# Group norm and attention on one core: the first normalising in two steps, copies of att in older bursts, and a product with v between two score tiles

## The chip, the core and the metric

The kernel runs on one core of one Trainium2 chip, in one launch. The metric is the device time of one execution in microseconds (us); lower is better. "Before" and "after" are compared by the medians of several executions.

## What is computed

```python
b, c, hh, ww = x.shape                  # 4, 512, 48, 48
t = hh * ww                             # 2304
d = c // num_heads                      # 64, with 8 heads
hn = _group_norm(x, gn_scale, gn_bias)  # 32 groups of 16 channels
qkv = jnp.einsum('oc,bchw->bohw', qkv_w, hn) + qkv_b[None, :, None, None]
qkv = qkv.reshape(b, 3, num_heads, d, t).astype(jnp.float16)
q, k, v = (qkv[:, 0], qkv[:, 1], qkv[:, 2])
scale = jnp.asarray(1.0 / math.sqrt(math.sqrt(d)), dtype=jnp.float16)
w = jnp.einsum('bhct,bhcs->bhts', q * scale, k * scale)
w = jax.nn.softmax(w, axis=-1)
a = jnp.einsum('bhts,bhcs->bhct', w, v).astype(jnp.float32)
a = a.reshape(b, c, hh, ww)
out = jnp.einsum('oc,bchw->bohw', proj_w, a) + proj_b[None, :, None, None]
return x + out
```

## The kernel before, in words

**Tiles.** The 512 channels are four chunks of 128 partitions (c = 0 to 3, `NC`). The 2304 positions are five query blocks (j = 0 to 4, `NQ`): four of 512 columns and a last one of 256. Two heads make a pair; there are four pairs to a batch and 16 pairs g in all. `hn[b, c, j]` holds x, and is normalised in place. All of the work is written out by hand in `fast_path`; each engine runs its instructions in the order in which they are issued there. (`general_path` is a fallback that doesn't run with these inputs.)

**The main loop.** `stream` lists 432 bursts (g, j, k). A burst is three score tiles `ps` of 128 x 1024: TensorE multiplies q and k of both heads (`scores`, L998), ScalarE takes the exponential of each tile into `p` (L1005). There are three `ps` buffers, so a score tile of one burst waits for the exponential of the tile with the same number in the burst before. Two bursts later (`BEHIND`) TensorE multiplies p with v (`values`, L1023) into the one PSUM bank `av`. VectorE adds the p of a block up (`add`, L1054; `join`, L1059). When a block (six bursts, or three for the short one) has ended, `avx` is copied out of the bank (L1032), the sums over keys are made in the same bank (`add_up`, L1082), copied out (`rows`, L1098), inverted and spread by DMA (L1101 to L1139), and GpSimd multiplies to give `att`, 16 bit (`divide`, L1147). For the last blocks of the whole kernel the division is done in place (`divide_here`, L1108 and L1109).

**Work beside the loop.** `beside` is a list of pieces in a planned order: projections to q and k (`qk_steps`, L748, evacuated by VectorE at L758), to v (`v_chain`, L799, L807), and the output projection of the batch before (`proj_run`, L887, with weights as a high and a low part, evacuated with bias and residual at L914, or at L910 where only the last pair's part is added, and stored at L919). They share one PSUM bank. `fill(n)` issues pieces as credit allows, each with an earliest burst (`after`); pieces of up to 0.1 us need no credit. It first runs `do_tasks`: small tasks of a loaded batch, with an allowance of 0 to 2.4 us to a burst: statistics (L621), `aggregate` (L625), `group_scale` (L635 to L647, and the power on GpSimd, L644), `coefficients` (L654 to L666) and `normalize` (L699).

**Copies of att.** The output projection needs `att` as 32 bit: `att32` makes four copies a block (one a pair), ScalarE the first two (L881) and GpSimd the last two (L879); where a `divide` was issued in the same burst, ScalarE makes three. They are issued at a block's `begin` piece. For blocks 2, 3 and 4 of the last batch (`in_two`) three pairs are projected early (`FIRST`: six matmuls a chain) and the last pair later (`LAST`). In the kernel before, `put_run(att32, b, j, FIRST, after=there)` copies all three pairs of such a block just ahead of its chains.

**Start.** While x is loaded, L1317 keeps TensorE busy with matmuls on ones. `all_stats(0)` takes the statistics of chunk 0; `first_group` (L678 to L691) averages them over the groups with two small matmuls on TensorE, raises to the power -1/2 on GpSimd (L686), and makes scale `ga` and bias `gb`. `norm_chunk` (L706) then normalises the five blocks of a chunk on ScalarE, block 0 first. Eight chains (k of five blocks, q of three) go through the chunks together, each in its own bank; the statistics of the next chunk stand among the coefficients of this one on VectorE.

**The last blocks.** `soon` holds the ends of blocks 2 and 3 of the last pair. After the loop come the last block's sums and the remaining chains of the output projection ("ahead", "rest", "held", "last_av").

Of the kernel before, what the change touches and what calls it, by code (L numbers as in the profile page):

```python
# [467 lines left out]
def fast_path(  # L468
# [201 lines left out]
    def first_group():  # L670

        mean, var = moments[:, 1, 0:1], moments[:, 2, 0:1]
        by = share.rearrange("p g j -> p (g j)")
        pm = small_bank("first_group")
        dev, var2, mg, veps, rstd = (
            small_tile(1, f"first_{n}") for n in ("dev", "var2", "mg", "veps", "rstd")
        )
        nc.tensor.matmul(pm[:, 0:1], by, mean, start=True, stop=True)  # L678
        nc.vector.tensor_tensor(dev, mean, pm[:, 0:1], ALU.subtract)
        nc.vector.tensor_scalar(var2, dev, dev, var, ALU.mult, ALU.add)  # L680
        nc.tensor.matmul(pm[:, 1:2], by, var2, start=True, stop=True)
        nc.vector.scalar_tensor_tensor(
            mg, pm[:, 0:1], -1.0, gsc[:, 0:1], ALU.mult, ALU.mult
        )
        nc.vector.tensor_scalar(veps, pm[:, 1:2], EPS, None, ALU.add)
        nc.gpsimd.tensor_tensor(rstd, veps, mhalf[:, 0:1], ALU.pow)  # L686

        def finish():
            ga, gb = small_tile(1, "first_ga"), small_tile(1, "first_gb")
            nc.vector.tensor_tensor(ga, rstd, gsc[:, 0:1], ALU.mult)  # L690
            nc.vector.tensor_scalar(gb, rstd, mg, gbi[:, 0:1], ALU.mult, ALU.add)  # L691
            ab[0, 0] = ga, gb

        return finish
# [5 lines left out]

    def norm_chunk(b, c):

        ga, gb = ab[b, c]
        for j in range(NQ):
            t = hn[b, c, j]
            nc.scalar.activation(t, t, AF.Identity, bias=gb, scale=ga)  # L706

# [156 lines left out]
    def att32(b, j, pairs=range(NC)):  # L867
        o, n = QBLOCKS[j]
        for c in pairs:
            if left_over(b, j):  # L870
                t = xpool.tile([P, n], F32R, tag=f"x{c}_{j}", name=f"a32_{b}_{j}_{c}")
            else:
                t = work.tile(
                    [P, QB], F32R, tag=f"a32_{c}", bufs=1, name=f"a32_{b}_{j}_{c}"
                )
            at32[b, j, c] = t[:, :n]
            source = atts[b * NPAIR + c][:, o : o + n]
            if c in beside_exps() and not (pairs == LAST and left_over(b, j)):
                nc.gpsimd.tensor_copy(at32[b, j, c], source)  # L879
            else:  # L880
                nc.scalar.copy(at32[b, j, c], source)  # L881
# [55 lines left out]
    def proj_pieces(b, j):  # L937
# [7 lines left out]
        def begin():  # L945
            att32(b, j, LAST if in_two(b, j) else range(NC))
            if j == 0:
                ahead(0)
                ahead(1)
# [36 lines left out]
    def scores(u):  # L986
# [5 lines left out]
        for r in range(BURST):  # L992
            ps = ps_s.tile([P, 2, QB], F32, tag="ps", name=f"ps_{g}_{j}_{k}_{r}")
# [172 lines left out]
    def reload(b, j):  # L1166


        def run():
# [4 lines left out]
            if j == NQ - 1:  # L1174

                tasks.append((n, 0.65, lambda: aggregate(b)))
                tasks.append((n, 1.2, lambda: group_scale(b)))
# [12 lines left out]
    def do_tasks(room):  # L1190
        while tasks and tasks[0][0] <= now[0] and room > 0:
            _, us, run = tasks.popleft()
            run()
            room -= us

# [35 lines left out]
    def put_first(b, j):  # L1231

        for jj, chunks in proj_list:
            if jj == j:
                put([proj_piece(b, j, chunks, FIRST)])

    for b in range(B):
# [20 lines left out]
        if b == B - 1:  # L1258
# [4 lines left out]

            ahead = [
# [4 lines left out]
            ]  # L1269
            for j in range(NQ):  # L1270
                put_proj(old, j, ahead)
                if j + 1 < NQ:
                    put_convert(old, j + 1)

            for j in (NQ - 2, NQ - 3, NQ - 1):
                there = ends[(NG - 2) * NQ + j] + BEHIND + 6
                put_run(att32, b, j, FIRST, after=there)
                put_first(b, j)
# [34 lines left out]
    idle = ps_av.tile([P, QB], F32, tag="av", name="idle")  # L1313

    def keep_busy(count):
        for _ in range(count):
            nc.tensor.matmul(  # L1317
                idle, busy[:, 0, :P], busy[:, 0, :], start=True, stop=True
            )

    def all_stats(c):
        for j in range(NQ):
            stats(0, j, c)
        aggregate(0, (c,))

    keep_busy(16)
    all_stats(0)
    first_coefficients = first_group()
    keep_busy(4)

    eight = [(1, j) for j in range(NQ)] + [(0, j) for j in range(8 - NQ)]
# [10 lines left out]
    for c in range(NC):  # L1342

        for j in range(NQ):
            if j == (1 if c < 2 else 2):
                if c == 0:
                    first_coefficients()
                else:
                    coefficients(0, (c,))
                norm_chunk(0, c)  # L1350
            if c + 1 < NC:
                stats(0, j, c + 1)
        if c + 1 < NC:
            aggregate(0, (c + 1,))
            group_scale(0, (c + 1,))
# [75 lines left out]
    for n in range(end):  # L1431
# [5 lines left out]
        scores(stream[n])  # L1437
# [6 lines left out]
        if summed:  # L1444

            fill(n)
        if n >= BEHIND:
# [9 lines left out]
        if not summed:  # L1457
# [158 lines left out]
```

## Time and profile before

| what | value |
|---|---|
| median of three runs | 1601.38 us (1600.72, 1601.38, 1603.44) |
| the profiled execution's own time | 1602.89 us |
| its span | 1601.2 us |
| TensorE: matmul busy | 1583.9 us (99%), 11524 instructions |
| ScalarE busy | 1268.1 us (79%) |
| VectorE busy | 1137.0 us (71%) |
| GpSimd busy | 327.9 us (20%) |
| granted TensorE clock, mean | 0.998 |

Times in the profile count from the start of the span. PE is TensorE (PEld its weight loads), ACT ScalarE, DVE VectorE, POOL GpSimd, SP SyncE, which issues DMAs. A row of the timeline gives start, time, engine, line, operation, output<-inputs, shapes and count; in brackets stands how long the engine had been idle, and what released it. Rows are merged where instructions of one kind follow each other. The end of a matmul is modelled, so the distance from one start to the next is the better measure for PE.

### The profile page before, as it was taken

The numbers are of one execution on the slowest core, as the hardware profiler recorded it, in microseconds if no ns is written. First come the engines' busy times: TensorE is split into PE (matmuls) and PEld (weight loads), VectorE is DVE, ScalarE is ACT, GpSimd is POOL, SyncE is SP. The second block draws the span as 40 slices with busy tenths as digits, with TensorE's granted clock in tenths as the row PEclk, the third lists the DMA queues.
The fourth block names the chain that finished last, engine by engine and source line by source line (L and its number), as shares of the span: only waits on it lengthen the run. The fifth ranks groups of instructions, "written<-read, shape, count | busy, mean of one in ns | idle before, by whom it ended". The sixth has DMA issues, their size and how long they took to land.

```text
span 1601.2 us, 28364 instructions
## 1 busy us (share of the span) xinstructions
PE 1583.9 (99%) x11524; PEld 695.0 (43%) x11524; DVE 1137.0 (71%) x1298; ACT 1268.1 (79%) x1362; POOL 327.9 (20%) x460
## 2 busy tenths in 40 slices
PE   9999999999999999999999999999999999999997
PEld 3533434443333534555333354445533334435554
DVE  6177668876666678887666666888767776766775
ACT  3177777888888888888888888877878888888895
POOL 1011212222121222222112111222212121111322
PEclk9999999999999999999999999999999999999999
DMA  7002020000000024521000001353101000015424
GB/s 217 8 14 67 11 71 17 18 15 12 14 18 15 9 70 119 145 64 28 11 15 18 14 12 41 111 154 90 25 15 18 15 15 11 15 31 163 151 67 128
DMA packets 94896, 82.10 MB, mean 51 GB/s; under 512 B 50852, under 2 KB 60964, under 8 KB 94756
## 3 DMA queue, kind: packets, MB, share of 16 engines
q1 hardware_dynamic: 92724, 78.35, 18.1%
q8 instruction: 92, 1.51, 0.4%
q10 hardware_dynamic: 1904, 1.84, 0.4%
q14 instruction: 48, 0.39, 0.1%
q0 software_dynamic: 128, 0.01, 0.0%
HBM read 60.70 MB, written 19.17 MB: 50 GB/s over the span
## 4 chain that ended last, share of the span: by engine, by line
PE 96%; DVE 1%; ACT 1%; DMA 1%; POOL 0%; issue 0%; SPq 0%; DVEq 0%
PE pqk L748 29%; PE ps L998 20%; PE av L1023 20%; PE pv L799 15%; PE pr L887 8%; PE sl L1082 2%; PE ps L748 1%; ACT p L1005 1%; DMA x<-x_dram 0%; DMA r<-x_dram 0%; DVE acc L1054 0%; PE first_av L748 0%; PE first_w L748 0%; DVE st L621 0%; POOL a L879 0%
## 5 line engine op out<-in xcount | busy, mean ns | idle before, releaser
L1005 ACT ACTIVATE p<-ps 128x1024 f16<-128x1024 f32 x1296 | 1233.3, 1025 | 302.5 <-PE ps L998 299.5
L1054 DVE TENSOR_TENSOR acc<-acc,p 128x3072 f16<-128x3072 f16 x270 | 487.2, 1805 | 54.0 <-ACT p L1005 51.6
L748 PE MATMUL pqk<-x,wqkv 128*64 128x512 f32 (+1 forms) x2432 | 510.2, 549 | 0.1
L1023 PE MATMUL av<-p,v 128*64 128x512 f16 (+1 forms) x2880 | 360.8, 364 | 0.4 <-DVE slx L1098 0.3
L998 PE MATMUL ps<-q,k 64*128 64x512 f16 (+1 forms) x2880 | 356.2, 358 | 1.5 <-ACT p L1005 1.1
L799 PE MATMUL pv<-wqkv,x 128*64 128x256 f32 x2304 | 267.5, 379 | 0.0
L748 PEld LDWEIGHTS pqk<-x,wqkv 128*64 128x64 f32 x2432 | 168.0, 137 | 205.9 <-issue 156.2
L1120 POOL TENSOR_SCALAR in<-sums 128x8 f32<-128x8 f32 (+1 forms) x158 | 101.3, 641 | 723.8 <-DMA sums<-slx 717.2
L998 PEld LDWEIGHTS <-k 64*128 64x128 f16 x2880 | 106.0, 94 | 288.5 <-issue 239.6
L1023 PEld LDWEIGHTS <-v 128*64 128x64 f16 x2880 | 131.3, 109 | 213.3 <-issue 168.6
L1147 POOL TENSOR_TENSOR att<-avx,ib 128x512 f16<-128x512 f32 (+1 forms) x78 | 126.5, 1622 | 434.2 <-DMA ib<-row 372.4
L799 PEld LDWEIGHTS pv<-wqkv,x 128*64 128x64 f32 x2304 | 161.7, 137 | 85.4
L1054 DVE TENSOR_TENSOR acc<-p,p 128x3072 f16<-128x3072 f16 x79 | 138.1, 1748 | 0.0
L887 PE MATMUL pr<-a,whi 128*128 128x512 f32 (+1 forms) x311 | 121.9, 399 | 2.6 <-DVE r L914 2.2
L1059 DVE TENSOR_TENSOR acc<-acc 128x1024 f16<-128x1024 f16 x156 | 112.5, 721 | 3.3
L887 PE MATMUL pr<-a,wlo 128*128 128x512 f32 (+1 forms) x311 | 113.6, 373 | 0.0
L758 DVE TENSOR_SCALAR k<-pqk,bqkv 128x512 f16<-128x512 f32 (+1 forms) x75 | 52.1, 695 | 77.4 <-PE pqk L748 77.2
L807 DVE TENSOR_TENSOR v<-pv,bv 128x512 f16<-128x512 f32 x72 | 49.6, 689 | 80.9 <-PE pv L799 80.8
L758 DVE TENSOR_SCALAR q<-pqk,bqkv 128x512 f16<-128x512 f32 (+1 forms) x77 | 53.4, 694 | 74.6 <-PE pqk L748 74.4
L1098 DVE COPY slx<-sl 128x512 f32<-128x512 f32 (+1 forms) x79 | 50.6, 640 | 66.0 <-PE sl L1082 66.0
L914 DVE SCALAR_TENSOR_TENSOR r<-pr,bproj,r 128x512 f32<-128x512 f32 (+1 forms) x80 | 54.9, 694 | 45.3 <-PE pr L887 40.2
L1032 DVE COPY avx<-av 128x512 f32<-128x512 f32 (+1 forms) x79 | 50.6, 640 | 38.5 <-PE av L1023 38.1
(102 smaller groups left out, 498.6 us busy)
## 6 DMA issues: line engine op xcount, KB each, us to landing
r<-x_dram SPq DMA_DIRECT2D x72, 256.0 KB, 3.6
out_dram<-r SPq DMA_DIRECT2D x69, 256.0 KB, 2.7
ib<-row SPq DMA_DIRECT2D x126, 128.0 KB, 3.1
x<-x_dram SPq DMA_DIRECT2D x62, 256.0 KB, 4.1
x<-x_dram SPq DMA_DIRECT2D x16, 128.0 KB, 5.0
sums<-slx SPq DMA_DIRECT2D x128, 2.0 KB, 2.1
ib<-row SPq DMA_DIRECT2D x30, 64.0 KB, 2.9
wqkv<-qkv_wT_dram SPq DMA_DIRECT2D x2, 768.0 KB, 6.9
```

What stands on the lines that cost most here:

```text
L748: nc.tensor.matmul(pw[0][lo : lo + D, :n], wqkv[:, c, w0 + lo : w0 + lo + D], hn[b, c, j], start=(c == 0), stop=(c == NC - 1),)
L758: nc.vector.tensor_scalar(qk[g][part][:, o : o + n], pw[0][:, :n], bqkv[:, col : col + 1], SCALE, ALU.add, ALU.mult,)
L799: nc.tensor.matmul(pw[0][lo : lo + D, a, :], hn[b, c, i * P // QB][:, at + lo : at + lo + D], wqkv[:, c, 2 * C + half * C // 2 :][:, : C / ...
L887: nc.tensor.matmul(ps[:, :n], w[:, c, bass.ts(m, P)], at32[b, j, c], start=(i == 0), stop=(i == len(steps) - 1),)
L914: nc.vector.scalar_tensor_tensor(xt[:, i], places[i], bias, xt[:, i], ALU.add, ALU.add)
L998: nc.tensor.matmul(ps[:, h, a * n : (a + 1) * n], kt[rows, bass.ts(i, P)], qt[rows, o : o + n], start=True, stop=True,)
L1005: nc.scalar.activation(pt[:, r], ps, AF.Exp)
L1023: nc.tensor.matmul(av[0][lo : lo + D, :n], vv[b, pr // 2][:, i, pr % 2 * P + lo : pr % 2 * P + lo + D], pt[:, r, h, a * n : (a + 1) * n], ...
L1054: nc.vector.tensor_tensor(t, before, pt, ALU.add)
L1059: nc.vector.tensor_tensor(t[:, 0], t[:, 0], t[:, r], ALU.add)
L1120: nc.gpsimd.tensor_scalar(t, sm, limit, None, op)
L1147: nc.gpsimd.tensor_tensor(atts[g][:, o : o + n], avx.pop((g, j))[:, :n], ibs.pop((g, j))[:, :n], ALU.mult,)
```

## The change

Five parts. In the start, `first_group` takes the mean of the variances by a matmul of its own, ahead of the deviations, and normalises in two steps: block 4 (256 columns) and block 0 of chunk 0 are multiplied by the channel's scale with the mean taken off while the power is still being computed, and by the power after it, block 4 on VectorE, block 0 on ScalarE; blocks 1 to 3 are done in one step as before. `next_group` does so with block 4 of the other chunks, on ScalarE. Chains and blocks start with block 4. The statistics of the next chunk come after all of this chunk's coefficients.

In the last batch, the copies of pairs 0 and 1 of blocks 3, 2 and 4, and of pair 2 of block 3, become pieces between the chains of the batch before; pair 2 of blocks 2 and 4 and pairs 0 and 1 of block 0 follow among the `FIRST` chains, those of block 0 on GpSimd. Pairs 0 and 1 of block 2 get tiles of their own.

`do_tasks` stops ahead of `group_scale` if a copy is due among the next two pieces.

In the loop, the product with v of the burst that ends block 3 of the last pair is issued between the second and the third score tile of a burst; and in the bursts that follow the two ends in `soon`, `fill` comes ahead of `values`.

```diff
-    def first_group():
+    def scale_bias(c, tag, col, mg):
+        ga, gb = (small_tile(1, f"{n}_{tag}") for n in ("ga", "gb"))
+        nc.vector.tensor_tensor(ga, col, gsc[:, c : c + 1], ALU.mult)
+        nc.vector.tensor_scalar(gb, col, mg, gbi[:, c : c + 1], ALU.mult, ALU.add)
+        ab[0, c] = ga, gb
+
+    def shifted(c, tag, mean):
+        mg = small_tile(1, f"mg_{tag}")
+        nc.vector.scalar_tensor_tensor(
+            mg, mean, -1.0, gsc[:, c : c + 1], ALU.mult, ALU.mult
+        )
+        return mg
+
+    def by_scalar(t, scale, bias):
+        nc.scalar.activation(t, t, AF.Identity, bias=bias, scale=scale)
+
+    def by_vector(t, scale, bias):
+        nc.vector.tensor_scalar(t, t, scale, bias, ALU.mult, ALU.add)
+
+    def first_group(meanwhile):
...
+        nc.tensor.matmul(pm, by, mean, start=True, stop=True)
+        nc.tensor.matmul(pv, by, var, start=True, stop=False)
+        nc.vector.tensor_tensor(dev, mean, pm, ALU.subtract)
+        nc.vector.tensor_tensor(dev2, dev, dev, ALU.mult)
+        nc.tensor.matmul(pv, by, dev2, start=False, stop=True)
+        mg = shifted(c, "a", pm)
+        small_first, then = hn[0, c, NQ - 1], hn[0, c, 0]
+        by_scalar(small_first, gsc[:, c : c + 1], mg)
+        by_scalar(then, gsc[:, c : c + 1], mg)
+        nc.vector.tensor_scalar(veps, pv, EPS, None, ALU.add)
         nc.gpsimd.tensor_tensor(rstd, veps, mhalf[:, 0:1], ALU.pow)
...
+        meanwhile()
+        by_vector(small_first, rstd, gbi[:, c : c + 1])
+        by_scalar(then, rstd, gbi[:, c : c + 1])
+        scale_bias(c, "a", rstd, mg)
+        for j in range(1, NQ - 1):
+            by_scalar(hn[0, c, j], *ab[0, c])
+
+    def next_group(c):
...
+        aggregate(0, (c,))
...
+        nc.gpsimd.tensor_tensor(rstd, veps, mhalf, ALU.pow)
+        means, mean_cols = small_tile(SQ, "means"), small_tile(SQ, "mean_cols")
+        nc.vector.tensor_copy(by_group(means), to_channels(grouped[:, :, 0]))
+        nc.vector.transpose(mean_cols, means)
+        mg = shifted(c, tag, mean_cols[:, c : c + 1])
+        first = hn[0, c, NQ - 1]
+        by_scalar(first, gsc[:, c : c + 1], mg)
+        scales, cols = small_tile(SQ, "scales"), small_tile(SQ, "cols")
+        nc.vector.tensor_copy(by_group(scales), to_channels(rstd))
+        nc.vector.transpose(cols, scales)
+        by_scalar(first, cols[:, c : c + 1], gbi[:, c : c + 1])
+        scale_bias(c, tag, cols[:, c : c + 1], mg)
+        for j in range(NQ - 1):
+            by_scalar(hn[0, c, j], *ab[0, c])
...
-    def att32(b, j, pairs=range(NC)):
+    EARLY = range(2)
+
+    def att32(b, j, pairs=range(NC), beside=None):
...
+            elif in_two(b, j) and c in EARLY:
+                t = xpool.tile(
+                    [P, n], F32R, tag=f"x{2 * c + 1}_1", name=f"a32_{b}_{j}_{c}"
+                )
...
-            if c in beside_exps() and not (pairs == LAST and left_over(b, j)):
+            if beside or c in beside_exps() and not (pairs == LAST and left_over(b, j)):
...
-            att32(b, j, LAST if in_two(b, j) else range(NC))
+            if in_two(b, j):
+                att32(b, j, LAST)
+            elif (b, j) == (B - 1, 0):
+                att32(b, j, range(len(EARLY), NC))
+            else:
+                att32(b, j)
...
-    def scores(u):
+    def scores(u, ahead_of_last=None):
...
         for r in range(BURST):
+            if r == BURST - 1 and ahead_of_last:
+                ahead_of_last()
...
-                tasks.append((n, 1.2, lambda: group_scale(b)))
+                power = lambda: group_scale(b)
+                powers.add(power)
+                tasks.append((n, 1.2, power))
...
     def do_tasks(room):
         while tasks and tasks[0][0] <= now[0] and room > 0:
+            if tasks[0][2] in powers and copies_next():
+                break
...
+    def copies_next():
+
+        return any(p[0] == 0.0 and p[5] <= now[0] for p in beside[:2])
...
-    def put_first(b, j):
+    def put_first(b, j, ahead):
 
         for jj, chunks in proj_list:
             if jj == j:
+                if ahead:
+                    put_run(*ahead.pop(0))
                 put([proj_piece(b, j, chunks, FIRST)])
...
+            THIRD = range(len(EARLY), NC - 1)
...
+            ahead += [
+                (att32, b, j, (c,)) for j in (NQ - 2, NQ - 3, NQ - 1) for c in EARLY
+            ]
+            ahead.append((att32, b, NQ - 2, THIRD))
             for j in range(NQ):
                 put_proj(old, j, ahead)
...
+            ahead = [
+                (att32, b, NQ - 3, THIRD),
+                (att32, b, NQ - 1, THIRD),
+                *((att32, b, 0, (c,), True) for c in EARLY),
+            ]
             for j in (NQ - 2, NQ - 3, NQ - 1):
-                there = ends[(NG - 2) * NQ + j] + BEHIND + 6
-                put_run(att32, b, j, FIRST, after=there)
-                put_first(b, j)
+                put_first(b, j, ahead if j != NQ - 2 else [])
...
-    eight = [(1, j) for j in range(NQ)] + [(0, j) for j in range(8 - NQ)]
+    first_group(meanwhile)
+
+    eight = [(1, j) for j in (NQ - 1, *range(NQ - 1))] + [(0, j) for j in range(8 - NQ)]
...
     for c in range(NC):
-
-        for j in range(NQ):
-            if j == (1 if c < 2 else 2):
-                if c == 0:
-                    first_coefficients()
-                else:
-                    coefficients(0, (c,))
-                norm_chunk(0, c)
-            if c + 1 < NC:
-                stats(0, j, c + 1)
         if c + 1 < NC:
-            aggregate(0, (c + 1,))
-            group_scale(0, (c + 1,))
+            for j in range(NQ):
+                if (j, c) != (0, 0):
+                    stats(0, j, c + 1)
+            next_group(c + 1)
...
-        scores(stream[n])
+        inside = n - BEHIND == soon[1]
+        scores(stream[n], (lambda: values(stream[n - BEHIND])) if inside else None)
...
-        if summed:
+        filled = summed or n - BEHIND - 1 in soon
+        if filled:
 
             fill(n)
-        if n >= BEHIND:
+        if n >= BEHIND and not inside:
             values(stream[n - BEHIND])
...
-        if not summed:
+        if not filled:
             fill(n)
```

## The prediction

> **What bounds the kernel.** I read the page first, then the waits of PE, then the starts in PE's timeline.
>
> ```profile
> span 1601.2 us, 28364 instructions
> ...
> PE 1583.9 (99%) x11524; PEld 695.0 (43%) x11524; DVE 1137.0 (71%) x1298; ACT 1268.1 (79%) x1362; POOL 327.9 (20%) x460
> ...
> PE 96%; DVE 1%; ACT 1%; DMA 1%; POOL 0%; issue 0%; SPq 0%; DVEq 0%
> ```
>
> PE is both the busy engine and the chain. The change removes no useful matmul, so it can gain only where PE stands still. The waits of PE name the places:
>
> ```profile
> PE pr L887 <- DVE r L914: 2.2, 1, 2.2
> ...
> PE ps L748 <- ACT x L706: 1.3, 1, 1.3
> PE ps L998 <- ACT p L1005: 1.1, 3, 0.5
> ...
> PE pr L887 <- POOL a L879: 0.4, 1, 0.4
> PE av L1023 <- DVE slx L1098: 0.3, 1, 0.3
> ...
> PE sl L1082 <- DVE avx L1032: 0.2, 1, 0.2
> ```
>
> The first row (at 1047 us) is a residual's DMA that lands late, behind loads of x. SP's queue holds the same instructions in the same order in both kernels, so I leave these 2.2 us. The others are what the change aims at. The timelines show them; first the start, with what leads to the first chain:
>
> ```profile
> 9.80 0.58 POOL L686 TENSOR_TENSOR first_rstd<-first_veps,mhalf 128x1 f32<-128x1 f32 x1 [4.69 <-DVE first_veps L685]
> ...
> 10.80 3.42 ACT L706 ACTIVATE x<-x,first_gb,first_ga 128x512 f32<-128x512 f32 x5 [4.60 <-DVE first_gb L691]
> ...
> 11.67 4.94 PE L748 MATMUL ps<-x,wqkv 128*64 128x512 f32 x24 [1.34 <-ACT x L706]
> ```
>
> then the power that stands ahead of a copy on POOL,
>
> ```profile
> 1067.35 0.71 POOL L644 TENSOR_TENSOR rstd<-veps,mhalf 128x2 f32<-128x2 f32 x1 [0.30 <-DVE both L647]
> 1068.02 2.12 POOL L879 CAST a<-att 128x512 fp32r<-128x512 f16 x1
> ```
>
> and three ACT copies in one gap with the score tile that waits for them, the product that waits for `slx`, and the third score tile among short bursts:
>
> ```profile
> 1512.73 1.67 ACT L881 CAST a<-att 128x512 fp32r<-128x512 f16 x3
> ...
> 1517.20 0.39 PE L998 MATMUL ps<-q,k 64*128 64x512 f16 x2 [0.30 <-ACT p L1005]
> ...
> 1562.07 0.84 PE L1023 MATMUL av<-p,v 128*64 128x512 f16 x6 [0.35 <-DVE slx L1098]
> ...
> 1579.00 0.39 PE L998 MATMUL ps<-q,k 64*128 64x256 f16 x4 [0.52 <-ACT p L1005]
> ```
>
> The gap in brackets understates a stall, as ends are modelled. So I price by starts: a burst's scores take 0.75 us from their start to the next group's (1513.18 to 1513.93); 1516.29 to 1517.52 is 1.23, a stall of 0.48.
>
> **What the Trainium skill says.** Perfetto Trace Analysis, "Identifying the Most-Contended Engine": matmul busy share is no good measure of room; one looks for gaps on the bounding engine. It agrees: 99% busy hides the 0.48 above in part. SBUF — State Buffer, "SBUF: two separate sides": DVE operations with two SBUF inputs and GpSimd reading SBUF lock one port pair for a whole instruction. The trace agrees: the POOL copy's median is 0.61 us, but 2.12 at 1068.02 beside `acc` (1067.92, 1.75 us). TensorEngine Tiling (Array Packing), "Key Properties": changing the tiling mode drains TensorE. The trace shows some 0.10 us a change: a product with v takes 0.77 before a projection with the 128*128 form (1513.93 to 1514.70), 0.67 before one in its own form (1102.24 to 1102.91).
>
> **1. The start.** In the row order of DVE: deviation ends at 8.70, `first_var` takes 8.74 to 9.01 (272 ns), PE starts its second matmul at 9.07, `veps` ends at 9.71 (behind `mg`), the power runs 9.80 to 10.38, `ga` and `gb` end at 10.77, ACT normalises block 0 from 10.80 to 11.62, PE starts at 11.67. After: the square is a plain tensor operation (155 ns, like the deviation): minus 0.12. `mg` no longer stands ahead of `veps`: minus 0.07. The power ends at 10.19. ACT's first passes cost nothing: `mg` is ready at 9.0, ACT has nothing else to do, block 4 takes 0.59 (L706's row for 256 columns), block 0 ends at about 10.3. The extra small matmul fills PE's wait (8.51 to 9.07). DVE then waits for the power, with `ga`, `gb` and the statistics behind it; block 4 costs 0.36 (least of L699), 10.22 to 10.58, so PE can start near 10.67. Its two half-width matmuls last 0.43. Block 0 needs ACT's second pass, behind its first: 10.33 to 11.14, plus 0.08: PE at 11.2, against 11.10 wanted. Blocks 1 to 3 follow at ACT's pitch of 0.71, under PE's 0.86. Start thus counts as 11.2 - 0.43 = 10.77: **0.9 us** of 11.67. The eight chains last 6.49 as before (11.67 to 18.16), so chunk 1 is wanted at 17.26. Its statistics are done 0.2 later than before; its power ends near 15.4, block 4's second pass near 16.5, block 0 at 17.3 against 17.69. Chunks 2 and 3 have over 0.9 spare. Here the cover is thinnest: half a microsecond more on DVE would eat into the gain. Bounds: 0.4 to 1.05. The rest of the prologue is one continuous PE chain (11.67 to 74 without a wait), so the gain stays.
>
> **2. The power after the copies.** Before, evacuation L914 stands behind DVE's norm operations (1065.35 to 1067.26) and frees the bank at 1068.01; the chain starts 0.14 late (1067.24 to 1068.15 is 0.91, not 0.77). Then the copy lands 0.57 late, and the restart costs 0.1 (the chain takes 2.71, not 2.06). After, the evacuation runs at 1066.6, the copy from 1067.1, since POOL's `att` ends at 1067.05. If `acc` blocks it until 1069.0 it lands by 1069.4, when its matmul is due (chain start 1068.01 plus 1.47). Gain **0.8**, bounds 0.2 to 0.82. The norm tasks come a burst later: `group_scale` (1.25 us) fits ahead of a chain's end; `coefficients` (1.08) push the next evacuation to end at about 1078.9 on this clock, against 1079.06 when the next chain needs the bank. I take 0, at worst 0.2 lost. POOL's power delays only DVE's `coefficients`. Normalised blocks are read from 1097 on, one to five bursts after they are ready.
>
> **3. Older bursts for the copies.** Gone from behind 1512.73 (three) and 1526.50 (two): 0.48 and, from 1529.58 to 1530.77, 1.19 - 0.75 = 0.44: **0.9 us**. There the period is 3.1 (0.75 + 0.77 + 1.59) against 2.85 of exponentials, so two copies (1.15) don't fit; in the older bursts it is 3.6, and a copy of 0.57 fits the 0.7 that ACT idles. One place gets three: behind p_4_2 at 1490.50. Its 1.67 push the exponentials to 1492.15 to 1495.0; the score tile that reuses the buffer is due at 1495.3. It fits by 0.3; the cost if not is 0.2 or so. GpSimd gets pair 2 of block 3 (idle until 1514) and block 0's pairs (idle from 1533.7 to 1544, where 1.2 to 2.8 is wanted). The copies need `att` and tiles that were free long before. No DMA moves. Bounds 0.4 to 0.92.
>
> **4. fill before values.** At 1560.90 scores to product is 1.17, 0.42 over 0.75: the product waits for `slx` (to 1562.02). With the chain (2.06) in between, it starts at 1563.7. The chain is ready: its copies end at 1561.30 (ACT) and 1561.48 (POOL), its bank at 1561.42, PE arrives at 1561.66. Behind it waits only the product. Gain **0.4**, bounds 0.2 to 0.42.
>
> **5. The product between two tiles.** Before: tiles 1 and 2 at 1577.85, tile 3 at 1579.00, product to 1580.09, chain, then `sl` 0.19 + 0.07 late. After: 0.76 + 0.77 and two more form changes (0.2 in all, by the 0.10 above, both bounds 0.1 and 0.3) end at 1579.6; the tile's buffer is free at 1578.94. The product ends by 1579.2, so `avx` is out before `sl` at 1580.3 (was 1581.02): 0.75. The chain ahead of the next product covers `slx` once more: 0.09. Behind, two paths meet at "rest" (1588.74): PE gains 0.84; `slx`, reciprocal (3.35), `att`, ACT copy gain 0.75. ACT isn't late: its exponentials of p_4_1 end at 1581.7, the third tile of p_4_2 is due at 1582.1. The last stores (from 1591.02) start with the work, so the end moves along: **0.8**, bounds 0.3 to 0.86.
>
> **Sum.** 0.9 + 0.8 + 0.9 + 0.4 + 0.8 = 3.8 us: 1602.89 - 3.8 = 1599.1 for the profiled execution (span 1597.4). That execution stood 1.5 above the median 1601.38, so the median should be 1597.6. Elsewhere pieces only trade places among bursts; groups of scores are 433 instead of 432 (priced in 5), of output projection 76 in both.
>
> **Rivals.** (A) All of it holds: 1597.6, own range 1596.4 to 1598.7; chance 0.68. (B) Covers are too thin: the two ACT passes start PE late (0.5 lost), the late evacuation costs 0.2, three copies bring a stall back (0.4), the split gives half (0.4): 3.8 - 1.5 = 2.3, 1599.1; chance 0.21. For it speak margins of 0.1 to 0.4; against it, that each is worked out with measured durations. (C) The cuts don't reach the end: the late part is absorbed by the final stores or a later residual (parts 3 to 5 lost): 3.8 - 2.1 = 1.7, 1599.7; 0.06. Against: the stores wait for PE. (D) Slower: postponed norm tasks leave VectorE behind. From 1050 to 1100 it is busy 45.5 of 50, 0.3 free a burst. A chain's bank must be free 1.52 after its end (0.75 + 0.77), so it decides where VectorE is over 0.8 late at the evacuation (0.67). At 0.8 more lost in nine chains, 7.2 go: 1597.6 + 7.2 = 1604.8; 0.05. Against: no task is added, only put one burst later.
>
> **Numbers.** 0.2% is 3.2 us, about what a measurement can tell here; the threshold is 1598.2. Runs of one kernel spread by 2.7. A falls below 1598.2 in most cases, B sometimes: faster 0.71, same 0.24, slower 0.05. The range 1596.2 to 1600.0 takes in A, B, C and the bounds.
>
> **What would show it.** Right: the first chain's start near 10.7 and no wait after block 0; PE at chunk 1 by 17.3; no row "PE pr <- POOL a" near 1066; scores at 0.75 throughout 1505 to 1545; no wait for `slx` or `avx`; "rest" 3.7 earlier. Wrong: a chain waiting for L914's counterpart near 1077, scores waiting near 1491, or a 1047 wait of another length, which would move the time without the change.

## The result, and the profile after

| kernel | median | range | ratio to before, with 95% interval |
|---|---|---|---|
| before, beside the changed one | 1601.45 us | 1600.72 to 1603.44, 13 runs | |
| changed | 1598.42 us | 1597.81 to 1599.32, 13 runs | 0.9977 (0.9970 to 0.9985) |

By the medians the change gains 3.0 us, 0.19%; the ratio puts it at 3.7 us, with an interval of 2.4 to 4.8. One run of each kernel (1650.17 us, and 1800.32 us at a granted clock of 0.85) is left out of range and ratio. The forecast was 1597.6, so by the medians 0.8 us of the gain is missing. That is less than the runs alone can tell, but the traces can. The profiled execution took 1598.20 us. From its page:

```profile
span 1596.5 us, 28388 instructions
...
PE 1582.6 (99%) x11526; PEld 695.0 (44%) x11526; DVE 1137.8 (71%) x1302; ACT 1269.4 (80%) x1363; POOL 338.0 (21%) x463
...
POOL 0%; DVE 0%; issue 0%; POOLq 0%
```

PE is 1.3 us less busy, and its share is the same 99%: as before, that line doesn't show where the time went. The chain now breaks off near its end (it follows POOL's last operations, not PE's), so that view has nothing to say. The waits of PE, with place, total, times and longest, do:

```profile
PE count L1626 <- DVE good L1625: 2.3, 1, 2.3
PE idle L1393 <- DVE busy L1389: 1.5, 1, 1.5
PE first_means L699 <- DVE moments L625: 0.7, 1, 0.7
PE ps L791 <- DVE x L687: 0.5, 1, 0.5
PE pv L842 <- DVE v L850: 0.3, 1, 0.3
PE ps L1054 <- DVE v L850: 0.3, 1, 0.3
PE first_vars L703 <- DVE first_dev L702: 0.2, 1, 0.2
PE pr L936 <- DVE r L963: 0.2, 1, 0.2
```

Gone are the rows for `p`, `slx`, `avx` and POOL's `a`; these are the stalls that the change aimed at (0.27 us for POOL's `a` is still there at 1545, as at 1548 before, too short for a row). Gone too is the residual's 2.2 us at 1047, which no part aims at. Two rows are new: a product for v (the projection to v, L842) that waits for evacuation L850 (0.3), and an output projection that waits for L963 (0.2). A stall is time in which PE stands still; I give every stall below as the excess of one start-to-start distance over the usual one, since the brackets understate it. The landing of x is the end of chunk 0's statistics; the flag is the last value that VectorE writes, and every engine reads it back to decide whether the fallback runs; I call the time from there to the end of the span the close. For the two profiled executions the account closes:

| place | us gained |
|---|---|
| start, from the landing of x to the first chain | 0.97, of which 0.85 remains at the first scores |
| landing of x | 0.25 |
| residual at 1047 | 2.23 |
| copy behind the power, 1067 | 0.82 |
| product for v, 1130 (new) | -0.49 |
| score tiles, 1516 and 1529 | 0.90 |
| projection, 1533 (new) | -0.28 |
| fill before values | 0.42 |
| product between two tiles | 0.85 |
| sum, at "rest" (1588.74 to 1583.20: 5.54) | 5.55 |
| from the flag to the end of the span: 6.36 before, 7.20 after | -0.84 |
| span, 1601.17 to 1596.47 | 4.7 |

The start in the timeline of the changed kernel, to be held against the rows of the prediction:

```profile
9.37 0.58 POOL L709 TENSOR_TENSOR first_rstd<-first_veps,mhalf 128x1 f32<-128x1 f32 x1 [4.26 <-DVE first_veps L708]
...
9.98 0.41 DVE L687 TENSOR_SCALAR x<-x,first_rstd,gbi 128x256 f32<-128x256 f32 x1
...
10.14 0.81 ACT L684 ACTIVATE x<-x,gbi,first_rstd 128x512 f32<-128x512 f32 x1
...
10.45 5.07 PE L791 MATMUL ps<-x,wqkv 128*64 128x256 f32 x24 [0.48 <-DVE x L687]
```

PE starts when DVE has done the narrow block. (One block's statistics of chunk 1, 9.20 to 9.88, stand ahead of that, in the wait for the power; the text on the change puts them all behind the coefficients.) ACT ends block 0's second pass at 10.95, and PE's next chain is 0.12 late for it. The tail, where the product now stands between the second and the third tile:

```profile
1556.64 0.82 PE L1054 MATMUL ps<-q,k 64*128 64x512 f16 x6
1557.39 0.50 PE L936 MATMUL pr<-a,whi 128*128 128x512 f32 x1
...
1573.16 0.63 PE L1054 MATMUL ps<-q,k 64*128 64x256 f16 x8
1573.72 0.84 PE L1079 MATMUL av<-p,v 128*64 128x512 f16 x6
1574.49 0.39 PE L1054 MATMUL ps<-q,k 64*128 64x256 f16 x4
1574.81 0.50 PE L936 MATMUL pr<-a,whi 128*128 128x512 f32 x1
```

From the scores at 1556.64 to the chain is 0.75, no stall; the three pieces of the split follow at 0.56, 0.77 and 0.32, none with a bracket.

Here is the first of the two new stalls. At 1130 PE's product for v wants the bank that `v` L850 empties:

```profile
1126.99 1.76 DVE L1110 TENSOR_TENSOR acc<-p,p 128x3072 f16<-128x3072 f16 x1
1128.66 1.36 DVE L753 TENSOR_SCALAR x<-x,ga,gb 128x256 f32<-128x256 f32 x1
1129.94 0.68 DVE L850 TENSOR_TENSOR v<-pv,bv 128x512 f16<-128x512 f32 x1
...
1127.59 2.28 POOL L1203 TENSOR_TENSOR att<-avx,ib 128x512 f16<-128x512 f32 x1 [5.16 <-DMA ib<-row]
...
1130.68 1.95 PE L842 MATMUL pv<-wqkv,x 128*64 128x256 f32 x16 [0.27 <-DVE v L850]
```

The normalising operation takes 1.36 us; the next one, alone, takes 0.38 (1132.30). It ends 0.15 us after POOL's `att` (1129.87), and the evacuation stands behind it. `att` itself is long: it starts while `acc` runs and takes 2.28 us, against 1.27 at 1528.89, where no `acc` had begun. In the kernel before, the order at this place was `acc`, evacuation, `acc`, and the two normalising operations had already run, ahead of it:

```profile
1128.26 0.73 DVE L699 TENSOR_SCALAR x<-x,ga,gb 128x256 f32<-128x256 f32 x2
...
1131.01 1.75 DVE L1054 TENSOR_TENSOR acc<-p,p 128x3072 f16<-128x3072 f16 x1
1132.68 0.68 DVE L807 TENSOR_TENSOR v<-pv,bv 128x512 f16<-128x512 f32 x1
...
1131.59 2.30 POOL L1147 TENSOR_TENSOR att<-avx,ib 128x512 f16<-128x512 f32 x1 [5.19 <-DMA ib<-row]
```

### The profile page after: what moved, and what is told of

The parts are those of the page before. It is cut to its first block, busy times and chain, and to the rows that moved or that the text cites. A ratio compares the mean times of both kernels' runs of the same rounds, so it can differ in the third digit from the quotient of the medians.

```text
span 1596.5 us, 28388 instructions
## 1 busy us (share of the span) xinstructions
PE 1582.6 (99%) x11526; PEld 695.0 (44%) x11526; DVE 1137.8 (71%) x1302; ACT 1269.4 (80%) x1363; POOL 338.0 (21%) x463
## 5 line engine op out<-in xcount | busy, mean ns | idle before, releaser
L842 PE MATMUL pv<-wqkv,x 128*64 128x256 f32 x2304 | 267.5, 379 | 0.3 <-DVE v L850 0.3
L1176 POOL TENSOR_SCALAR in<-sums 128x8 f32<-128x8 f32 (+1 forms) x158 | 106.2, 672 | 713.3 <-DMA sums<-slx 706.8
L1203 POOL TENSOR_TENSOR att<-avx,ib 128x512 f16<-128x512 f32 (+1 forms) x78 | 131.3, 1683 | 423.7 <-DMA ib<-row 372.3
L842 PEld LDWEIGHTS pv<-wqkv,x 128*64 128x64 f32 x2304 | 161.6, 137 | 86.0 <-DVE v L850 0.8
L850 DVE TENSOR_TENSOR v<-pv,bv 128x512 f16<-128x512 f32 x72 | 49.7, 690 | 80.9 <-PE pv L842 80.8
L963 DVE SCALAR_TENSOR_TENSOR r<-pr,bproj,r 128x512 f32<-128x512 f32 (+1 forms) x80 | 54.9, 695 | 42.2 <-PE pr L936 39.8
```

What stands on the lines that cost most here:

```text
L842: nc.tensor.matmul(pw[0][lo : lo + D, a, :], hn[b, c, i * P // QB][:, at + lo : at + lo + D], wqkv[:, c, 2 * C + half * C // 2 :][:, : C / ...
L963: nc.vector.scalar_tensor_tensor(xt[:, i], places[i], bias, xt[:, i], ALU.add, ALU.add)
L1176: nc.gpsimd.tensor_scalar(t, sm, limit, None, op)
L1203: nc.gpsimd.tensor_tensor(atts[g][:, o : o + n], avx.pop((g, j))[:, :n], ibs.pop((g, j))[:, :n], ALU.mult,)
```

## The experiments

The missing 0.8 us has two candidates of about its size: the new stalls (0.49 + 0.28), or the close of the program, which gave back 0.84. The experiments come in three groups; each group was measured beside the kernel before, whose median was 1601.85, 1601.54 and 1601.70 us in them. So medians of different groups differ by some tenths without any cause in the kernels, and single stalls are read from the traces. The first group takes parts out and puts parts in alone.

**start_alone.** The kernel before with `first_group`, `next_group` and the order of blocks of the changed one, and nothing else:

```diff
-    first_coefficients = first_group()
-    keep_busy(4)
+    first_group(meanwhile)
...
-    eight = [(1, j) for j in range(NQ)] + [(0, j) for j in range(8 - NQ)]
+    eight = [(1, j) for j in (NQ - 1, *range(NQ - 1))] + [(0, j) for j in range(8 - NQ)]
```

> The kernel before with the new start alone (two-step normalising, block 4 first). Theory, that every part keeps in the whole what it gains alone: the first chain starts at 10.5 us and chunk 1 at 17.1 (before 18.16), then no gap of PE up to the first product, so 0.85 to 1.1 us less, about 1600.5. The stalls at 1067 (0.8), 1516 and 1529 (0.9), 1560 (0.4) and 1580 (0.5) stay as before, a microsecond earlier. Rival, that the earlier start is lost later in the prologue or at the loads of x: PE waits again before 100 us and the time is that of before within 0.3 us. On the residual at 1047 (2.2 us in the profile before): if its stall is chance of the loads, it may be there or not; if the other parts took it away, it is here in full.

Measured: 1600.50 us against 1601.85 of the kernel before; ratio 0.9992 (0.9985 to 0.9998). The medians say 1.35, more than the start itself gains. In its profile x landed late (statistics done at 8.14), so the clock times mislead; from there to the first scores of the stream it is 64.91 us, against 65.75. Over all twelve profiles this distance is 65.75 or 65.76 in the five with the old start and 64.90 or 64.91 in the seven with the new: the start is worth 0.85 us, wherever x lands (7.71 to 8.14), and the rival falls. The stalls at 1067, 1516, 1529, 1560 and 1580 are there as expected; the one at 1047 is not, though no part is there that could have removed it.

**split_and_fill.** The kernel before with the tail's two parts:

```diff
-        scores(stream[n])
+        inside = n - BEHIND == soon[1]
+        scores(stream[n], (lambda: values(stream[n - BEHIND])) if inside else None)
...
-        if summed:
+        filled = summed or n - BEHIND - 1 in soon
+        if filled:
             fill(n)
```

> The kernel before with the last two parts alone: the product with v between two score tiles of the last short burst, and the fill ahead of the values there. First theory for the microsecond that the forecast has too much, the new stalls at 1130 (0.49) and 1533 (0.28): the last piece of PE starts 1.3 us earlier than before and the time falls by as much, about 1600.2. Second theory, that the close of the program gives back what the last stage gains: the last PE piece starts 1.3 us earlier, but from the flag to the end of the span it takes 7.2 us and not 6.4, and the time falls by 0.4 at most, about 1601.

Measured: 1600.98 against 1601.85; ratio 0.9995 (0.9986 to 1.0003), which doesn't tell 1.3 from 0.4. The profile does. No stall is left between 1549 and 1586; "rest" is 2.13 earlier, of which 0.90 is a shorter stall at 1047 (1.33) and 1.23 the tail. The close took 6.96. In start_alone, whose tail is that of the kernel before, it took 7.26. The row of the flag's load on SP (nanoseconds, least, median, most) shows 0.62 of the 0.84, first before, then after:

```profile
L1571 SPq TENSOR_LOAD <-flag x1: 295/295/295, 1594.8 to 1594.8; - x1
```

```profile
L1642 SPq TENSOR_LOAD <-flag x1: 917/917/917, 1589.3 to 1589.3; - x1
```

The flag is the same tile in both; where the other 0.2 lies is open. In the twelve profiles the close is 6.36 once and 6.82 to 7.41 otherwise, four of these with the old tail (6.82, 6.95, 7.26, 7.41). The 0.84 is thus a short close of the profiled execution before, not a price of the change: the second theory falls.

**no_yield.** The changed kernel without the break in `do_tasks`:

```diff
-            if tasks[0][2] in powers and copies_next():
-                break
```

> The changed kernel without the yield: the norm's power and what follows it run when due, ahead of copies of att. First theory: the stall before the projection at 1067 is back with 0.8 us and the one before the product for v at 1130 (0.49) is gone, since the norm tasks run a burst earlier again; the sum is 0.3 us slower than the changed kernel, about 1598.7. Rival, that the stall at 1130 comes from something else (the block that starts there, or the earlier start): it stays, and the kernel is 0.8 us slower, about 1599.2.

Measured: 1598.44, ratio 0.9978 (0.9969 to 0.9988): the time of the changed kernel. At 1064 POOL has the old order again:

```profile
1061.49 1.63 POOL L1203 TENSOR_TENSOR att<-avx,ib 128x512 f16<-128x512 f32 x1 [5.94 <-DMA ib<-row]
1063.89 0.72 POOL L644 TENSOR_TENSOR rstd<-veps,mhalf 128x2 f32<-128x2 f32 x1 [0.76 <-DVE both L647]
1064.56 2.12 POOL L928 CAST a<-att 128x512 fp32r<-128x512 f16 x1
```

The stall is back (0.14 + 0.58 + 0.11 = 0.83), and the one at 1130 is gone, as the first theory has it: the yield breeds it. Of the two forecasts, 1598.7 and the rival's 1599.2, the first is the nearer. Not expected: the stalls at 1533 (0.28) and at 1545 (0.27) are gone too in this execution, with the same order of instructions there. They hang on a few tenths of timing; and this execution, 1597.64 us, is the fastest of the ten, so it stands for the median less well than others.

**pairs_at_begin.** The changed kernel with block 0's two early copies back at its begin:

```diff
-            elif (b, j) == (B - 1, 0):
-                att32(b, j, range(len(EARLY), NC))
...
-                *((att32, b, 0, (c,), True) for c in EARLY),
```

> The changed kernel with block 0's first two copies of the last batch back where they were, on ACT with the other two at the block's begin; the third pairs' copies stay in older bursts. First theory: the stall of 0.28 us before the projection at 1533, put down to acc held up by the two POOL copies, is gone, and the score tile that waits behind ACT's copies in the gap near 1529 is late again by 0.4: 0.15 us slower than the changed kernel, about 1598.6. Rival, that the stall at 1533 is due to the product att on POOL beside acc, not to the copies: 0.28 stays and 0.4 comes on top, about 1598.8. If the score tile is not late (other copies have left the gap), it is 0.28 faster than the changed kernel, 1598.1.

Measured: 1598.05, ratio 0.9975 (0.9965 to 0.9985): the third case. The score tile near 1529 is not late, and the stall at 1533 is gone. So these two copies on POOL bring nothing, and in the profile of the changed kernel they cost 0.28. How they do it is not quite what I wrote. The changed kernel:

```profile
1528.89 1.27 POOL L1203 TENSOR_TENSOR att<-avx,ib 128x512 f16<-128x512 f32 x1 [3.75 <-ACT p L1061]
1530.11 3.16 POOL L928 CAST a<-att 128x512 fp32r<-128x512 f16 x2
...
1529.36 2.42 DVE L1110 TENSOR_TENSOR acc<-acc,p 128x3072 f16<-128x3072 f16 x1
1531.81 0.98 DVE L1115 TENSOR_TENSOR acc<-acc 128x1024 f16<-128x1024 f16 x1
1532.72 0.74 DVE L963 SCALAR_TENSOR_TENSOR r<-pr,bproj,r 128x512 f32<-128x512 f32 x1
...
1533.51 0.51 PE L936 MATMUL pr<-a,whi 128*128 128x512 f32 x1 [0.21 <-DVE r L963]
```

and the experiment:

```profile
1529.29 1.27 POOL L1201 TENSOR_TENSOR att<-avx,ib 128x512 f16<-128x512 f32 x1 [3.78 <-ACT p L1059]
...
1529.73 2.44 DVE L1108 TENSOR_TENSOR acc<-acc,p 128x3072 f16<-128x3072 f16 x1
1532.21 0.69 DVE L1113 TENSOR_TENSOR acc<-acc 128x1024 f16<-128x1024 f16 x1
1532.82 0.74 DVE L963 SCALAR_TENSOR_TENSOR r<-pr,bproj,r 128x512 f32<-128x512 f32 x1
```

`acc` takes 2.4 us instead of 1.75 in both: that is `att`'s doing, and it is hidden. The copies stretch the join behind it (0.98 against 0.69), and these 0.29 us are what PE waits. Both delays are needed, as the profiles suggest: in no_yield `att` came earlier, `acc` took 2.12, and the same join of 0.98 cost nothing.

The second group tries the cause of the stall at 1130, and what the residual at 1047 is worth. That residual stands on SP's queue as follows (kernel before):

```profile
1035.46 0.38 SPq L1129 DMA_DIRECT2D row<-inv  x1
1035.93 1.84 SPq L512 DMA_DIRECT2D x<-x_dram  x4
1040.18 1.12 SPq L1139 DMA_DIRECT2D ib<-row  x2
1041.39 0.54 SPq L919 DMA_DIRECT2D out_dram<-r  x1
1041.97 0.42 SPq L850 DMA_DIRECT2D r<-x_dram  x1
```

`ib` waits until `row` has landed; everything behind it waits along, and the residual itself then took 6.89 us to land.

**before_residual_early.** The kernel before, each residual loaded one chain earlier, so ahead of the loads of x:

```diff
                 ahead(1)
+                ahead(2)
...
-            proj_piece(b, j, chunks, pairs, lambda k=k: ahead(k + 2))
+            proj_piece(b, j, chunks, pairs, lambda k=k: ahead(k + 3))
```

> The kernel before, with each residual of a projection loaded one chain earlier; nothing of the change is in it. Theory: the third residual of a batch stands on SP's queue behind eight loads of x, behind ib, which waits for the landing of row, and behind a store; how late it lands is the chance of the DMA queues, and the stall at 1047 (2.2 us in one profile of this order, 1.3 in another, 0 in a third) with it. Loaded ahead of the loads of x it is there in time: no stall at 1047, the runs lie within about 1.5 us instead of 3.7, and the median falls by some 0.8 us, to about 1601.0, near the least of the kernel before. Rival, that the scatter of the kernel before is that of the program's close and of the granted clock: the profile may be without the stall, but the runs scatter as before and the median stays within 0.3 us.

Measured: 1601.37 against 1601.54 (ratio 1.0, 0.9991 to 1.0008), from 1600.91 to 1603.41. The stall is gone from the profile, but the median moves by 0.17 only, and the scatter stays: my theory on the scatter falls. Over the profiles with the old order of loads the stall is 2.23 (before), 1.33 (split_and_fill), 0.40 (yield_alone) and twice 0 in the old kernel's relatives, 0.32 (pairs_at_begin) and three times 0 in the changed kernel and its own: it varies from one execution to the next, and in the median it is small.

**hold_narrow.** pairs_at_begin, and the last block's normalising operations skip the burst in which `att` is put:

```diff
+                        if jj == NQ - 1:
+                            narrow.add(run)
...
+            if tasks[0][2] in narrow and ended(now[0] - BEHIND - 4):
+                break
             _, us, run = tasks.popleft()
```

> The changed kernel with block 0's pairs copied at the block's begin, and with the narrow normalising operations (256 columns, the last block) held back in the burst four behind a block's end, in which POOL's product att is put; the yield stays. Theory, that the stall of 0.49 us before the product for v at 1130 comes from a normalising operation that stands ahead of the evacuation while att has the port pair: x_2_4 now stands behind the evacuation, this starts at about 1128.7 instead of 1129.9, the stall is gone, and the kernel takes 1597.6. Rival, that the evacuation itself or acc is stretched by att: the operation behind acc is held for the same 0.7 us whichever it is, the stall stays at 0.3 or more, and the time is that of the kernel with the pairs at the begin, 1598.05.

Measured: 1597.67, ratio 0.9976 (0.9966 to 0.9985), as the theory has it. At the same place:

```profile
1127.11 1.76 DVE L1108 TENSOR_TENSOR acc<-p,p 128x3072 f16<-128x3072 f16 x1
1128.79 0.68 DVE L850 TENSOR_TENSOR v<-pv,bv 128x512 f16<-128x512 f32 x1
1129.39 2.22 DVE L1108 TENSOR_TENSOR acc<-acc,p 128x3072 f16<-128x3072 f16 x1
...
1127.83 2.17 POOL L1201 TENSOR_TENSOR att<-avx,ib 128x512 f16<-128x512 f32 x1 [5.27 <-DMA ib<-row]
```

`att` holds POOL as long as before, but the evacuation runs its usual 0.68 beside it, and what is stretched is the next `acc` (2.22), which nobody waits for. This is what the Trainium skill has on SBUF — State Buffer, "Who interferes with whom": a `tensor_scalar` within SBUF can be in a mode that takes the port pair shared with GpSimd, so it blocks for the other's whole instruction, while an operation with at most one input in SBUF does not contend outside such modes. The evacuation, one of whose inputs is a PSUM bank, agrees (0.68 beside `att`), and so does the normalising operation (1.36, not 0.38); that it is in such a mode is inferred from this stretch alone. The rival, that whatever stands behind `acc` is held, falls. Both new stalls are gone in this kernel: PE takes 2.50 us from the product with v (1129.69) to the scores behind the product for v, against 2.99 in pairs_at_begin and in the changed kernel. The median is the 1597.6 of the forecast, but it doesn't show this step by itself: pairs_at_begin belongs to another group, and the two ratios (0.9975 and 0.9976) don't differ.

**hold_narrow_residual_early.** The two edits above together.

> The kernel of the run before this one, with each residual loaded one chain earlier as well. Theory: the stall at 1047 is small or absent in most executions of the changed kernel and its relatives (0, 0 and 0.3 us in three profiles), so that the median falls by 0.1 to 0.3 us, to about 1597.4, and the scatter to under 1 us. Rival, that the changed order of the loads only moves the lateness (a residual's load waits for a store to land and holds up x, ib or sums behind it on SP's queue): a new stall of a residual or of POOL's att shows, and the time is 0.3 us or more above that of the run before.

Measured: 1597.46, from 1597.29 to 1597.84; ratio 0.9974 (0.9964 to 0.9985). No stall of a residual is left, none is new, and the eight runs lie within 0.55 us. The stall at 1545, which this edit doesn't touch, is absent here as well and present in hold_narrow. It is the fastest kernel of the study, by 1.0 us below the changed one.

The third group tests the sum of the parts and the yield.

**copies_alone.** The kernel before with the early copies of the last three blocks:

```diff
+            ahead += [
+                (att32, b, j, (c,)) for j in (NQ - 2, NQ - 3, NQ - 1) for c in EARLY
+            ]
+            ahead.append((att32, b, NQ - 2, THIRD))
...
-                put_run(att32, b, j, FIRST, after=there)
-                put_first(b, j)
+                put_first(b, j, ahead if j != NQ - 2 else [])
```

> The kernel before with the earlier copies of att for the last batch's last three blocks alone (pairs 0 to 2 in older bursts, block 0's copies at its begin). Theory, that each part keeps what it gains alone: the stalls of the score tiles at 1516 (0.47) and 1529 (0.43) are gone and nothing takes their place, 0.9 us less, about 1600.7. Rival, that part of what looked like the start's and the tail's gain is the copies': 1.5 us or more. Second rival, that the copies' gain needs the other parts, since DVE or ACT is late elsewhere when they run: under 0.3 us. On the scatter of the kernel before (1600.6 to 1604.3), which the changed kernel hasn't: if it is bred where ACT's copies stand in the score tiles' way, it is under 2 us here.

Measured: 1601.08 against 1601.70, from 1599.98 to 1602.6; ratio 0.9992 (0.9983 to 1.0). In its waits of PE the scores wait for `p` only once, in the tail (three times before, 1.1 us):

```profile
PE ps L1007 <- ACT p L1014: 0.5, 1, 0.5
```

The stalls at 1516 and 1529 are gone and nothing takes their place: 0.90 us by the profile, and the first theory holds. The scatter is 2.6 us, so the copies are not what breeds it.

**yield_alone.** The kernel before with the break in `do_tasks`:

```diff
+            if tasks[0][2] in powers and copies_next():
+                break
```

> The kernel before with the yield alone. Theory, that the norm's tasks a burst later trade one stall for another: 0.82 us at 1067 gone, 0.49 at 1130 new, 0.3 us less, about 1601.2, hardly to be told from no change. Rival, that the stall at 1130 needs the earlier start or the other parts: 0.8 us less, about 1600.7.

Measured: 1601.21 against 1601.70; ratio 1.0 (0.9991 to 1.0008), no difference that the runs can tell. By the profile: no stall at 1067, and a new one of 0.39 at 1131 with the normalising operation at 1.36 again. So the trade needs no other part. By the medians the four parts alone gain 1.35 (start), 0.87 (tail), 0.62 (copies) and 0.49 (yield); only the start's interval excludes no change, so the sum of the parts rests on the stalls in the traces.

**best_no_yield.** hold_narrow_residual_early without the yield and without the holding back:

```diff
-            if tasks[0][2] in powers and copies_next():
-                break
...
-            if tasks[0][2] in narrow and ended(now[0] - BEHIND - 4):
-                break
```

> The last kernel of the call before (pairs at the block's begin, residuals one chain earlier) without the yield and without the holding back of narrow operations. Theory: the yield is worth 0.8 us once the stall that it breeds at 1130 is held off: the stall at 1067 is back, there is none at 1130, and the time is 1598.2 to 1598.3 against 1597.46. Rival, that the yield is worth nothing, as the changed kernel and the one without it took the same time: 1597.5.

Measured: 1598.40, from 1597.79 to 1598.6; ratio 0.9978 (0.9969 to 0.9988). That is 0.94 above the kernel with both, which belongs to the second group; against the kernel before, each in its own group, the two gain 3.30 and 4.08, 0.78 apart. With its side effect held off, the yield is worth what step 2 gave it, 0.8. The profile shows the 0.81 of 1064 (0.14 + 0.56 + 0.10), and 0.26 at 1545 that comes and goes.

## Why the prediction was right, and where it was off

The forecast, faster by 3.8 us with case A the likeliest, was right in direction, and its five gains are measured within 0.05 us each. The time is 0.8 us above it, for two costs that were entered at nothing. The prediction gave 0.71 to a median below 1598.2, the size that it held a measurement could tell; 1598.42 is just above, so of its own three outcomes the likeliest did not come. By the number alone case B (1599.1) is as near as case A (1597.6); that the five gains are there in full decides for A.

- **The start.** 0.9 forecast, 0.85 measured in seven profiles. The first chain starts at 10.45 where 10.7 was expected; 0.25 of it is an earlier landing of x, so the working was right within 0.03. Chunk 1 starts at 17.06, ready in time.
- **The power after the copies.** 0.8 forecast, 0.82 measured at 1067; evacuation and copy run at 1063.2 and 1063.3 (3.35 later on the clock of before: the evacuation at 1066.6 as forecast, the copy half a microsecond earlier), and POOL stands free. The failed term is the one behind it, "I take 0, at worst 0.2 lost": it is 0.49 (0.39 in yield_alone). I looked for the price of postponing in the next chains (1077), where the evacuation was indeed in time, and on DVE's own load. It lay sixty microseconds on, where a normalising operation, one burst later than before, falls ahead of an evacuation and beside `att`, and is held for 1.0 us. That is case D's late evacuation behind a postponed norm task, at one place where D had nine, and through a hold by GpSimd where D had VectorE's load.
- **Older bursts.** 0.9 forecast and measured; the three copies behind p_4_2 (1486.87, 1.67 us) fit. But block 0's pairs on GpSimd were entered at nothing, as "idle from 1533.7": the engine was free, DVE beside it was not. That is -0.28 in this execution, and these two copies were not needed at all.
- **fill before values.** 0.4 forecast, 0.42 measured. **The product between two tiles.** 0.8 forecast, 0.85 measured. The two extra form changes were entered at 0.2 and cost 0.12: the scores take 0.56 + 0.32 where an unsplit group takes 0.76 (1570.97 to 1571.73).
- **The end.** "The end moves along": it does. Case C, that the cuts don't reach the end, seemed half true in the two profiles (0.84 given back), and was the chance of one execution.
- **The residual at 1047.** I left its 2.2 us in, and they are gone in the profile after. That the stall stays was wrong: how late that load lands varies with the execution. So the forecast for the profiled execution, 1599.1, was missed the other way (1598.20), by luck. For the profiled execution the sum reads 3.8 + 2.23 + 0.25 - 0.84 - 0.77 = 4.67, against 4.70 of the spans; 0.77 are the two new stalls, and the only part of the miss that belongs to the change.

The change's own terms make 0.85 + 0.82 + 0.90 + 0.42 + 0.85 - 0.77 = 3.07, and the medians 3.03. That they agree so closely is partly luck: the median of the kernel before alone lies between 1601.45 and 1601.85 in the four comparisons. That the new stalls cost these 0.77 is shown by the traces, in which pairs_at_begin removes the one and hold_narrow both; the median of hold_narrow, 1597.67, agrees.

What stays open: executions of the old kernel and its relatives scatter by 2.4 to 4.2 us and those of the changed one by 0.5 to 1.8. The late residual doesn't explain it. The upper runs of the old kernel and its relatives mostly have a mean granted clock of 0.996 or 0.997 and the lower ones 0.998 (beside the third group the kernel before takes 1603.14 on average at 0.997, 1601.27 at 0.998); but in pairs_at_begin, with the new parts, runs at 0.997 take no longer (1598.06 against 1598.09). Which is cause and which effect no run here tells. It moves the medians of the old kernel by some tenths, and may be part of the 3.0.

## What to carry to other kernels

When a step is postponed, follow everything that is queued behind it to its new place, and ask there which evacuation it will precede and which engine shares a port with it; "one burst later" cost nothing at the next projection chains (1071 to 1090) and 0.49 us at 1130. An idle engine is not a free place for work: GpSimd's two copies cost 0.28 us through a join on VectorE in the profiled execution, and gained nothing. And before a difference of two profiles is given to a change, compare the same stretch over several profiles: the landing of x, one residual and the close of the program moved by 0.4, 2.2 and 1.05 us between executions without any edit there.

## What the runs showed of the hardware

- Beside GpSimd's product `att` a normalising operation of 256 columns takes 1.36 us instead of 0.38, and `acc` 2.1 to 2.4 instead of 1.75; `att` that starts while `acc` runs takes 2.28 instead of 1.27. But the evacuation of v, with an input from PSUM, takes 0.67 to 0.69 in every one of its 63 executions from 75 us on, in each of the twelve profiles, three to five of them beside `att`. Which of them stands at that moment decides whether it costs anything.
- From the flag to the end of the span it is 6.36 to 7.41 us; the flag's load on SP takes 0.30 in one execution and 0.88 to 0.94 in the eleven others.
- Two more changes of PE's form between 64*128 and 128*64 cost 0.12 us where a product stands between two score tiles (0.56 + 0.32 against 0.76).
